# Norms in pieces, finished by GpSimd, in a four-layer transformer kernel; what a stage begins with is made by sequence in the preceding stage

## The chip, the cores and the metric

The kernel runs on one core of a Trainium2 chip, in one launch. The metric is the device time of that core in microseconds (us); lower is better. The core's engines run side by side, each with its own instruction queue: PE (TensorE, matrix products and transposes; PEld is its weight load), DVE (VectorE), ACT (ScalarE), POOL (GpSimd) and SP (SyncE, here a queue for transfers).

## The reference, cut to what matters

The input x is 4 sequences of 512 tokens with 128 channels, f32. There are four layers, and each of them does

```python
x = x + 0.5 * ffn(norm(x))
x = x + attn(norm(x))
x = x + 0.5 * ffn(norm(x))          # norm: (x - mean) / sqrt(var + 1e-5) over the 128 channels
```

- Layer 0: ffn is a mixture of 8 gelu-gated experts (top 2, limited capacity), attention has 16 heads with one projection for queries, keys and values.
- Layer 1: ffn is a dense gated chain with ternary weights (512 hidden units, a silu gate and two gelu products); attention is a running weighted mean (cumulative sums of exp(k) k and exp(k)) whose input is normalized a second time with gamma and beta.
- Layer 2: ffn is a mixture in which each of 8 experts chooses 256 of the 2048 tokens; attention is linear (elu + 1).
- Layer 3: ffn is a top-1 mixture of three-layer experts; attention is softmax with 16 heads.

## The kernel before, in words

x stays in SBUF as four tiles of 128 tokens by 128 channels for each of four sequences. Weights come by transfer ahead of their stage. A scheduler orders the instructions of each engine from the program's dependences and its own estimates; where the code wants another order, `after(ins, before, ...)` adds a dependence for the scheduler only, without a wait on the chip. `in_turn` does that for PE: between two settings of it all PE work is issued in the program's order, except in `out_of_turn()`. A generator is a piece of work that is cut into steps: `step(pieces, n)` advances the first of a list of generators by n steps, `run` finishes one. `latest["ins"]` is the newest instruction of the main chain, which `behind_latest` puts something behind.

**Norms.** `layer_norm` (L220) does a whole norm of one sequence on DVE: four `bn_stats` (L228), four `bn_aggr` (L230), `inverse_root` (L202) on a 128x4 tile, and four scalings `xn` (L240). `inverse_root` is 4 small instructions (v, i, y, h: L210 to L213) and three Newton steps of 3 instructions (t, t, y: L215 to L217). `twice=True` (layer 1's attention) adds a second inverse root. `norm_in_pieces` (L246) is the same, cut into steps, used in layer 0's attention. `transposed` (L268) makes the transposes of a norm on PE and copies them by ACT.

**Layer 0.** `l0_route` (L356) makes norms, router logits, softmax and the slots of half of the tokens (1024); `slack` adds empty steps. `l0_dispatch` scatters rows to slots by indirect transfers, `l0_experts` (L488) does up and down products of 8 experts per half, `l0_gather` (L574) gathers the results back by indirect transfers on POOL, paced by memsets. In the attention, `scores` (L838) does 256 blocks of 128 queries; `ops.row_max` is a product (smax) and a maximum on DVE (mp, L695), `ops.weigh` a second product (sexp) and an exponential on ACT. `begin(c)` makes the norm and transposes of sequence c, `take_apart` splits projected queries into bf16 parts on POOL (partsq, restq), and `load` brings these to the layout of the products by transfers (rows, queries).

**Layer 1.** `l1` (L977) works on pairs of sequences, twice (first and second ffn), so there are four rounds. A round is, for its two sequences, `first` (products p, tiles ha_a), `hidden` with weights th1 (products pb), `hidden` with th2 (products pc), and in the next round `leave` (product po, which also adds to x). Each 128x512 tile of activations is split into three bf16 parts, h, hr and hl (`Parts.take_apart`, L966); hl (L969) is on POOL for even o and on DVE for odd. Beside it, in steps: `begin(k, b)`, the norm xn_g and transposes ps_g of a sequence that comes next, and `attention(b)`, with norm xn_a, transposes ps_a, products pk, pka and pv, two scans, and transposes po_a.

**Layers 2 and 3.** `l2_ffn` and `l3_ffn` begin with a norm of each sequence, its transposes and router logits lg, in tiles that belong to the stage, then the softmax or the choice of all 2048 tokens. They end with transfers that bring the result (`yt`, in layer 2 also x) and adds to x. `l2_attn` and `l3_attn` begin with `begin(b)` or `enter(b)`, a norm and transposes of each sequence, and end with the residual of each sequence.

Of the kernel before, what the change touches and what calls it, by code (L numbers as in the profile page):

```python
# [9 lines left out]
F32 = mybir.dt.float32  # L10
# [73 lines left out]
def kernel(  # L84
# [117 lines left out]
    def inverse_root(var, n, name, bufs=4):  # L202


        def tmp(tag, dt=F32):
            return small.tile([P, n], dt, tag=f"ir_{tag}{n}", bufs=bufs, name=f"ir_{tag}_{name}")

        v, h, t, y = (tmp(i) for i in ("v", "h", "t", "y"))
        i = tmp("i", I32)
        nc.vector.tensor_scalar(v, var, EPS, None, op0=ALU.add)  # L210
        nc.vector.tensor_scalar(i, v.bitcast(I32), 1, None, op0=ALU.logical_shift_right)
        nc.vector.tensor_scalar(y.bitcast(I32), i, -1.0, float(0x5F3759DF), op0=ALU.mult, op1=ALU.add)
        nc.vector.tensor_scalar(h, v, -0.5, None, op0=ALU.mult)  # L213
        for _ in range(3):
            nc.vector.tensor_tensor(t, y, y, op=ALU.mult)  # L215
            nc.vector.tensor_tensor(t, t, h, op=ALU.mult)
            nc.vector.scalar_tensor_tensor(y, t, 1.5, y, op0=ALU.add, op1=ALU.mult)  # L217
        return y

    def layer_norm(pool, src, name, bufs=2, width=D, twice=False):  # L220
# [11 lines left out]
        if twice:  # L232

            v2 = small.tile([P, TT], F32, tag="ln_v2", name=f"v2_{name}")
            nc.vector.tensor_tensor(v2, rs, rs, op=ALU.mult)
            nc.vector.tensor_tensor(v2, v2, mv[:, :, 1], op=ALU.mult)
            r2 = inverse_root(v2, TT, f"2{name}")
            nc.vector.tensor_tensor(rs, rs, r2, op=ALU.mult)
# [7 lines left out]
    def norm_in_pieces(pool, src, name, bufs=1):  # L246

        st = small.tile([P, TT, 6], F32, tag="ln_st", name=f"st_{name}")
        mv = small.tile([P, TT, 2], F32, tag="ln_mv", name=f"mv_{name}")
        xn = pool.tile([P, TT, D], F32, tag="xn", bufs=bufs, name=f"xn_{name}")  # L250
        for t in range(TT):
            nc.vector.bn_stats(out=st[:, t, :], in_=src[:, t, :])
            if t % 2:
                yield
        for t in range(TT):
            nc.vector.bn_aggr(out=mv[:, t, :], in_=st[:, t, :])
        yield
        rs = inverse_root(mv[:, :, 1], TT, name)
        yield
        for t in range(TT):  # L260
            nc.vector.tensor_scalar(
                xn[:, t, :], src[:, t, :], mv[:, t, 0:1], rs[:, t : t + 1], op0=ALU.subtract, op1=ALU.mult
            )
            if t % 2:
                yield
        return xn
# [14 lines left out]
    def softmax(pool, lg, n, name):  # L281
# [7 lines left out]
        nc.vector.tensor_reduce(out=mx, in_=lg, axis=AX.X, op=ALU.max)  # L289
        nc.vector.tensor_tensor(sh, lg, wide(mx, NE), op=ALU.subtract)  # L290
        nc.scalar.activation(ex, sh, AF.Exp)
        nc.vector.tensor_reduce(out=sm, in_=ex, axis=AX.X, op=ALU.add)
        nc.vector.reciprocal(rc, sm)
        nc.vector.tensor_tensor(pr, ex, wide(rc, NE), op=ALU.mult)
        return pr

    def first_largest(pool, v, n, name, dt=F32):
# [6 lines left out]
        nc.vector.tensor_reduce(out=mx, in_=v, axis=AX.X, op=ALU.max)  # L304
        nc.vector.tensor_tensor(eq, v, wide(mx, NE), op=ALU.is_equal)
        nc.vector.tensor_tensor(eq, eq, first, op=ALU.mult)
        nc.vector.tensor_reduce(out=m2, in_=eq, axis=AX.X, op=ALU.max)
        nc.vector.tensor_tensor(oh, eq, wide(m2, NE), op=ALU.is_equal)
# [47 lines left out]
    def l0_route(wk, k, half, in_memory=True, slack=0):  # L356
# [9 lines left out]
        for i in range(8):  # L366
            nc.vector.bn_stats(out=st[:, i, :], in_=tiles[i])
            if i % 4 == 3 or slack:
                yield
        for i in range(8):  # L370
            nc.vector.bn_aggr(out=mv[:, i, :], in_=st[:, i, :])
        yield
        rs = inverse_root(mv[:, :, 1], 8, nm)
        if slack:
            yield
        for i in range(8):
            nc.vector.tensor_scalar(
# [7 lines left out]
        for h in range(2):  # L385
# [10 lines left out]
            nc.vector.tensor_copy(lgs[:, 4 * h : 4 * h + 4, :], lg)  # L396
            yield
        raw = softmax(wk, lgs, 8, f"r{nm}")
        yield
        m1 = first_largest(wk, raw, 8, f"a{nm}", BF16)  # L400
        yield
        rest = tmp([P, 8, NE], "rest")
        nc.vector.tensor_tensor(rest, raw, m1, op=ALU.mult)
        nc.vector.tensor_tensor(rest, raw, rest, op=ALU.subtract)
        m2 = first_largest(wk, rest, 8, f"b{nm}", BF16)
# [15 lines left out]
        nc.vector.scalar_tensor_tensor(kept[0], p1, float(C0), m1, op0=ALU.is_lt, op1=ALU.mult)  # L421
        nc.vector.tensor_tensor(row[:, 0], p1, place, op=ALU.add)
# [11 lines left out]
        nc.vector.tensor_tensor(gate[:, 0], raw, kept[0], op=ALU.mult)  # L434
        nc.vector.scalar_tensor_tensor(kept[1], p2, float(C0), m2, op0=ALU.is_lt, op1=ALU.mult)
        nc.vector.tensor_tensor(row[:, 1], p2, place, op=ALU.add)
        yield
        nc.vector.tensor_tensor(gate[:, 1], rest, kept[1], op=ALU.mult)
        for i in range(2):
            nc.vector.tensor_tensor(row[:, i], row[:, i], kept[i], op=ALU.mult)  # L440


        if not in_memory:

            pos = tmp([P, 2, 8, NE], "pos")
            for i, p in enumerate((p1, p2)):
                nc.vector.scalar_tensor_tensor(pos[:, i], p, 1.0, kept[i], op0=ALU.add, op1=ALU.mult)
            again = tmp([P, 8, NE], "again")
            nc.vector.tensor_tensor(again, pos[:, 1], kept[0], op=ALU.mult)
            nc.vector.tensor_tensor(pos[:, 1], pos[:, 1], again, op=ALU.subtract)  # L450
            nc.vector.tensor_tensor(pos[:, 0], pos[:, 0], pos[:, 1], op=ALU.add)
# [5 lines left out]
        nc.vector.tensor_reduce(out=rw, in_=row, axis=AX.X, op=ALU.add)  # L457
        nc.vector.tensor_scalar(idx, rw, float(T2), None, op0=ALU.add)
        nc.vector.tensor_reduce(out=gt, in_=gate, axis=AX.X, op=ALU.add)
        nc.vector.tensor_scalar(gt, gt, 0.5, None, op0=ALU.mult)  # L460
# [15 lines left out]

    latest = {}

    def behind_latest(ins):
        after(ins, latest["ins"], "not in front of work that its data would hold up")  # L480
# [93 lines left out]
    def l0_gather(wk, k, half, y_d, blanks=0):  # L574
# [6 lines left out]
        def pieces(s):  # L581
# [11 lines left out]
            for _ in range(4):  # L593
                yield
# [152 lines left out]
    def l0_attn(lp):  # L747
# [11 lines left out]
        def begin(c):  # L759
            xn = yield from norm_in_pieces(lp, x[:, c], f"a0_{c}")  # L760
# [52 lines left out]
        def prepare():  # L813
# [5 lines left out]
            for i in range(2):  # L819
# [3 lines left out]
                yield  # L823
            values(0)
# [13 lines left out]
        def scores(wk, rt, aside):  # L838
# [57 lines left out]
            take_apart(2, nc.gpsimd)  # L896
# [6 lines left out]
            for s4 in range(AHEAD // 4, 64 + 17):  # L903
                for half in range(2):
# [6 lines left out]
                    if (s4, half) == (45, 0):  # L911
                        aside.append(l0_route(rt, 1, 0, in_memory=False, slack=2))
# [11 lines left out]
                    if 0 < i < 17:  # L924
# [4 lines left out]
                        if slot == 3 and i < 15:  # L929
# [47 lines left out]
    def l1(aside, then):  # L977
# [3 lines left out]
        pieces = list(aside)  # L981

        with tc.tile_pool(name="l1f", bufs=1, reuse_waits="tile") as wk, \
             tc.tile_pool(name="l1a", bufs=2, reuse_waits="tile") as wa:

            def begin(k, b):
                nm = f"{k}_{b}"
                xn = layer_norm(wk, x[:, b], f"g{nm}")
                yield
# [8 lines left out]
            def first(k, b):  # L998
                nm = f"{k}_{b}"
                act[b] = Parts(wk, 4, "h", 4, f"a{nm}")  # L1000
                for o in range(4):
# [12 lines left out]
                    latest["ins"] = act[b].take_apart(o, nc.gpsimd if o % 2 == 0 else None)  # L1014
                    step(pieces)

            def hidden(k, b, w, sc, name):
                nm = f"{k}_{b}"
                given, act[b] = act[b], Parts(wk, 4, "h", 4, f"{name}{nm}")
                for o in range(4):  # L1020
# [8 lines left out]
                    latest["ins"] = act[b].take_apart(o, nc.gpsimd if o % 2 == 0 else None)  # L1029
                    step(pieces)  # L1030
# [22 lines left out]
            def attention(b):  # L1053
# [8 lines left out]
                xn = layer_norm(wa, x[:, b], f"a1_{b}", twice=True)  # L1062
                yield
# [22 lines left out]
                yield  # L1086
# [10 lines left out]
            for b in (0, 1):  # L1097
                run(begin(0, b))
            last = ()
            for k in range(2):  # L1100
                for p in ((0, 1), (2, 3)):
                    for b in p:
                        if last:
                            leave(*last.pop(0))
                            if k + p[0] and not (k == 1 and p[0] == 2):
                                pieces.append(attention((b + 2) % 4))
                        first(k, b)
                    for b in p:
                        hidden(k, b, th1, hs1, "b")
                    if (k, p[0]) == (0, 0):  # L1110
                        for r in pieces:
                            run(r)
                        pieces.clear()
                        then()
                    nk, nb = (k, 2) if p[0] == 0 else (k + 1, 0)
                    if nk < 2:
# [3 lines left out]
                    for r in pieces:  # L1120
                        run(r)
                    pieces.clear()
                    last = [(k, b) for b in p]
            for r in last:
                leave(*r)

# [14 lines left out]
    def l2_ffn(k):  # L1141
        W = D + NE
        with tc.tile_pool(name=f"l2f{k}", bufs=1, reuse_waits="tile") as wk:
# [7 lines left out]
            xd = dram.tile([T, W], F32, tag=f"xd2{k}", name=f"xd2_{k}")  # L1151
            sums_of[k, 0] = dram.tile([T, D], F32, tag=f"s{k}0", name=f"sum_{k}_0")
            xns = []
            lg = acc_bank([P, NT, NE], f"lg2_{k}")
            for b in range(B):
                xn = layer_norm(wk, x[:, b], f"c{k}_{b}", bufs=B, width=W)
                xns.append(xn)
                xT = transposed(wk, xn[:, :, :D], f"c{k}_{b}")
                for t in range(TT):
                    matmul(  # L1160
# [842 lines left out]
```

## Time and profile before

| | |
|---|---|
| time, median of 3 runs (lowest, highest) | 1688.43 us (1686.02, 1689.11) |
| profiled execution, time | 1685.38 us |
| profiled execution, span | 1683.3 us |
| mean granted clock of PE | 0.88 |
| instructions | 24707 |

The profile is of one execution. A window's row gives the span and then each engine's busy time in that stretch (with the number of instructions), the clock granted to PE (1 is full speed), the busy share of the DMA engines and the rate. In a timeline row the first number is the start, the second the duration; the bracket tells how long the engine had been idle and what released it. A row of groups ends with busy time, mean duration in ns, and the idle time before the group. The stages of the span, in us:

| stretch | stage |
|---|---|
| 0 to 181 | layer 0, first ffn (routing, then two halves of experts) |
| 181 to 436 | layer 0, attention |
| 436 to 580 | layer 0, second ffn |
| 580 to 872 | layer 1, four rounds: to 645, 727, 809, 872 |
| 872 to 992 | layer 2, first ffn (router to 888) |
| 992 to 1034 | layer 2, attention |
| 1034 to 1153 | layer 2, second ffn (router to 1048) |
| 1153 to 1290 | layer 3, first ffn (router to 1176) |
| 1290 to 1545 | layer 3, attention (entry to 1316) |
| 1545 to 1683 | layer 3, second ffn (router to 1563) |

### The profile page before, as it was taken

The numbers are of one execution on the slowest core, as the hardware profiler recorded it, in microseconds if no ns is written. First come the engines' busy times: TensorE is split into PE (matmuls) and PEld (weight loads), VectorE is DVE, ScalarE is ACT, GpSimd is POOL, SyncE is SP. The second block draws the span as 40 slices with busy tenths as digits, with TensorE's granted clock in tenths as the row PEclk, the third lists the DMA queues.
The fourth block names the chain that finished last, engine by engine and source line by source line (L and its number), as shares of the span: only waits on it lengthen the run. The fifth ranks groups of instructions, "written<-read, shape, count | busy, mean of one in ns | idle before, by whom it ended". The sixth has DMA issues, their size and how long they took to land.

```text
span 1683.3 us, 24707 instructions
## 1 busy us (share of the span) xinstructions
PE 1364.7 (81%) x8372; PEld 851.1 (51%) x8372; DVE 1036.7 (62%) x3225; ACT 666.1 (40%) x1411; POOL 563.3 (33%) x756
## 2 busy tenths in 40 slices
PE   3999889989899987979992637373785899998685
PEld 2898524334489834444551525253684233333685
DVE  5447677888445688989856357724214788884311
ACT  1333457767532323433320212020342377775242
POOL 0444245231345171313210631072684200100585
PEclk9999779999999998989995868575797599998698
DMA  8022211111311000004020230123543423310345
GB/s 318 30 62 61 49 44 52 49 42 33 119 59 47 21 23 36 1 1 188 15 63 27 36 66 26 30 40 84 177 148 120 95 52 71 69 33 22 102 183 187
DMA packets 97145, 121.26 MB, mean 72 GB/s; under 512 B 12224, under 2 KB 85429, under 8 KB 95482
## 3 DMA queue, kind: packets, MB, share of 16 engines
q1 hardware_dynamic: 76393, 69.84, 14.5%
q0 software_dynamic: 15968, 44.98, 9.0%
q10 hardware_dynamic: 4656, 4.86, 0.8%
q8 instruction: 66, 1.08, 0.3%
q14 instruction: 62, 0.50, 0.1%
HBM read 91.88 MB, written 27.79 MB: 71 GB/s over the span
## 4 chain that ended last, share of the span: by engine, by line
PE 60%; DVE 15%; POOL 8%; DMA 7%; issue 6%; ACT 2%; SPq 1%; POOLq 0%; ACTq 0%; DVEq 0%
PE pa L162 9%; PE av L162 7%; PE po L162 7%; PE smax L162 6%; PE sexp L162 6%; PE pc L162 5%; PE pb L162 4%; PE lg L162 2%; POOL y L1584 2%; DMA sum<-y,idx 2%; DVE mp L695 2%; POOL paced L334 2%; PE p3b L162 2%; PE p L162 1%; PE pq L162 1%
## 5 line engine op out<-in xcount | busy, mean ns | idle before, releaser
L695 DVE TENSOR_REDUCE mp<-smax 128x1 f32<-128x512 f32 (+1 forms) x512 | 326.5, 683 | 63.6 <-PE smax L162 61.4
L733 ACT ACTIVATE e<-sexp 128x512 f32<-128x512 f32 x512 | 272.0, 599 | 116.5 <-PE sexp L162 112.0
L162 PE MATMUL smax<-keys,queries 72*128 72x512 bf16 x512 | 204.1, 410 | 12.4 <-DMA queries<-rows_q 4.6
L162 PE MATMUL sexp<-queries,keys 75*128 75x512 bf16 (+1 forms) x512 | 195.7, 393 | 13.8 <-DVE mp L695 12.3
L520 ACT ACTIVATE gl<-pa 128x256 f32<-128x256 f32 x160 | 61.2, 383 | 157.9 <-PE pa L162 112.3
L162 PEld LDWEIGHTS <-th 128*128 128x128 bf16 x768 | 73.9, 96 | 97.1 <-issue 4.2
L162 PEld LDWEIGHTS <-queries 72*128 72x128 bf16 x512 | 52.3, 103 | 139.5 <-issue 88.3
L1533 POOL DMA_INDIRECT xg<-xd,src x46 | 46.8, 1018 | 175.0 <-DVE wi L1523 167.7
L521 DVE TENSOR_TENSOR hid<-pa,gl 128x256 f32<-128x256 f32 x160 | 67.1, 423 | 55.4 <-ACT gl L520 45.2
L162 PEld LDWEIGHTS po<-we,hid 128*128 128x128 f32 x768 | 90.5, 192 | 2.1
L162 PE MATMUL po<-we,hid 128*128 128x128 f32 x768 | 90.8, 275 | 0.0
L587 POOL DMA_INDIRECT yg<-y,idx x64 | 66.4, 1037 | 52.7 <-DMA y<-y 42.0
L162 PE MATMUL pa<-xTe,we 128*128 128x256 f32 (+1 forms) x352 | 81.7, 381 | 1.0 <-DVE xTe L509 1.0
L162 PE MATMUL pa<-ei,we 128*128 128x256 f32 (+1 forms) x352 | 81.3, 385 | 1.3 <-DVE hid L521 0.7
L162 PEld LDWEIGHTS <-keys 75*128 75x128 bf16 (+1 forms) x512 | 50.5, 101 | 55.5 <-issue 18.0
L162 PE MATMUL av<-e,v 128*32 128x512 f32 x512 | 72.6, 639 | 0.0
L334 POOL MEMSET paced<- 128x256 f32 x218 | 71.8, 329 | 0.3
L162 PEld LDWEIGHTS pa<-ei,we 128*128 128x128 f32 (+1 forms) x352 | 65.8, 192 | 10.7 <-DVE hid L521 1.4
L162 PEld LDWEIGHTS pa<-xTe,we 128*128 128x128 f32 (+1 forms) x352 | 64.5, 189 | 11.9 <-issue 1.4
L162 PE MATMUL av<-e,vp 128*32 128x512 f32 x512 | 69.6, 612 | 0.0
L165 PE MATMUL ps_a<-cst,xn_a 128*128 128x128 f32 x64 | 14.9, 354 | 58.0 <-DVE xn_a L240 58.0
L162 PE MATMUL p3b<-h3a,wd 128*128 128x128 f32 x480 | 60.3, 281 | 0.0
(428 smaller groups left out, 2915.0 us busy)
## 6 DMA issues: line engine op xcount, KB each, us to landing
we<-in_w0p_dram SPq DMA_DIRECT2D x8, 1080.0 KB
we<-in_e_pack_dram SPq DMA_DIRECT2D x8, 963.0 KB
queries<-rows SPq DMA_DIRECT2D x48, 96.0 KB
queries<-rows_q SPq DMA_DIRECT2D x48, 96.0 KB
y<-y SPq DMA_DIRECT2D x32, 128.0 KB
xd<-xn_c SPq DMA_DIRECT2D x8, 272.0 KB
slots<-zero ACTq DMA_DIRECT2D x2, 1024.0 KB
xs<-slots SPq DMA_DIRECT2D x16, 128.0 KB
```

The lines of the kernel that those rows point to most:

```text
L162: return turn_of(nc.tensor.matmul(*a, **k))
L165: return turn_of(nc.tensor.transpose(*a, **k))
L334: zeros = nc.gpsimd.memset(paced, 0.0)
L520: nc.scalar.activation(gl, pa[:, 0], AF.Gelu_apprx_tanh)
L521: latest["ins"] = nc.vector.tensor_tensor(hids[e][:, c, :], pa[:, 1], gl, op=ALU.mult)
L587: m = nc.gpsimd.indirect_dma_start(out=yg[:, t, i], out_offset=None, in_=y_d[:, :], in_offset=rows_in(idx[:, i, t : t + 1]), bounds_check= ...
L695: return nc.vector.tensor_reduce(out=self.mp[i][:, t, j], in_=s, axis=AX.X, op=ALU.max, negate=True)
L733: return e, nc.scalar.activation(e, s, AF.Exp, scale=scale)
L1533: m = nc.gpsimd.indirect_dma_start(out=xg[i], out_offset=None, in_=xd[:, :], in_offset=rows_at(src, i), bounds_check=T - 1, oob_is_err=False,)
L1584: m = nc.gpsimd.indirect_dma_start(out=y_d[:, :], out_offset=rows_at(to, i), in_=y, in_offset=None, bounds_check=T - 1, oob_is_err=False,)
```

## The change

- `inverse_root` and `norm_in_pieces` take an engine. With `eng=nc.gpsimd`, DVE does the statistics and v, i and y; GpSimd does h, the Newton steps (four instructions each instead of three) and the four scalings. The DVE part of these norms, of routing and of its softmax is issued through `behind`, which puts each instruction behind `latest["ins"]` for the scheduler.
- Layer 0: norms 2 and 3 of the attention and the route beside it are finished by GpSimd; the third block's queries are taken apart in the preparation and loaded at the start of the scores. Routing of the second half goes through `behind` too.
- Layer 1: norms of the second pair of the first ffn, all of the second ffn and all attention norms are in pieces and finished by GpSimd. Attention generators have lists of their own. hl is on POOL for all o where a round is not the first, and for even o only in product c of the first round, none earlier. The load of resident constants goes behind the first round's product c.
- A class `Router` does the first part of the ffns of layers 2 and 3 (store of x or of the norm, norm, transposes, logits) for one sequence; the preceding stage runs it (`r2.enter`, `r3.enter`), in layer 1's last round for sequences 0 and 1 on GpSimd. `l2_ffn` and `l3_ffn` issue all loads of their end first and then the adds, and call `then(b)` after each. Layer 2's and 3's attention norms go the same way.

The core of the diff:

```diff
-    def inverse_root(var, n, name, bufs=4):
+    def inverse_root(var, n, name, bufs=4, vector=None, eng=None):
...
+        on = eng or vector
+        on.tensor_scalar(h, v, -0.5, None, op0=ALU.mult)
         for _ in range(3):
+            on.tensor_tensor(t, y, y, op=ALU.mult)
+            on.tensor_tensor(t, t, h, op=ALU.mult)
+            if eng:
+                on.tensor_scalar(t, t, 1.5, None, op0=ALU.add)
+                on.tensor_tensor(y, y, t, op=ALU.mult)
+            else:
+                on.scalar_tensor_tensor(y, t, 1.5, y, op0=ALU.add, op1=ALU.mult)
...
+    def norm_in_pieces(pool, src, name, bufs=1, eng=None, twice=False, width=D, tag="xn"):
...
+            (eng or behind).tensor_scalar(
+                xn[:, t, :D], src[:, t, :], mv[:, t, 0:1], rs[:, t : t + 1], op0=ALU.subtract, op1=ALU.mult
             )
...
@@ layer 0, attention
-            xn = yield from norm_in_pieces(lp, x[:, c], f"a0_{c}")
+            xn = yield from norm_in_pieces(lp, x[:, c], f"a0_{c}", eng=nc.gpsimd if c > 1 else None)
...
-                        aside.append(l0_route(rt, 1, 0, in_memory=False, slack=2))
+                        aside.append(l0_route(rt, 1, 0, in_memory=False, slack=3, eng=nc.gpsimd))
...
@@ layer 1
+                xn = yield from norm_in_pieces(
+                    wk, x[:, b], f"g{nm}", bufs=2, eng=nc.gpsimd if k + b // 2 else None
+                )
+                for _ in range(4):
+                    yield
...
-                    latest["ins"] = act[b].take_apart(o, nc.gpsimd if o % 2 == 0 else None)
-                    step(pieces)
+                    low = k or b > 1 or name == "c" and o % 2 == 0
+                    latest["ins"] = act[b].take_apart(o, nc.gpsimd if low else None)
+                    go_on()
...
-                xn = layer_norm(wa, x[:, b], f"a1_{b}", twice=True)
-                yield
+                xn = yield from norm_in_pieces(wa, x[:, b], f"a1_{b}", bufs=2, eng=nc.gpsimd, twice=True)
+                for _ in range(2):
+                    yield
...
+                            if (k, p[0]) == (1, 2):
+                                pieces.append(enter(b - 2, nc.gpsimd))
+                            else:
+                                attending[b % 2].append(attention((b + 2) % 4))
...
+            for k, b in last:
+                run(enter(b))
...
@@ routers of layers 2 and 3
+        def enter(self, b, eng=None):
...
+            xT = transposed(nxt, xn[:, :, :D], nm, bufs=B)
+            yield
+            lg = acc_bank([P, TT, NE], f"lg{nm}")
+            for t in range(TT):
+                matmul(
+                    lg[:, t, :], lhsT=xT[:, t * P : (t + 1) * P], rhs=take(mat, MAT, f"wr{layer}"),
+                    start=True, stop=True,
+                )
...
@@ layer 3, attention
+                    if slot == 0 and i in (2, 6):
+                        enters.append(l3_enter(xTs, i // 4 + 2, nc.gpsimd))
+                    with out_of_turn():
+                        step(aside if i >= 16 else enters)
...
@@ the stages in their order
-    l2_ffn(0)
-    l2_attn()
-    l2_ffn(1)
+    begin, rest = l2_attn()
+    l2_ffn(0, r2, lambda b: begin(b) if b == 0 else None)
+    r2 = Router(1, 2)
+    rest(r2.enter)
+    r3 = Router(0, 3)
+    l2_ffn(1, r2, lambda b: run(r3.enter(b)))
     early.close()
-    l3_ffn(0)
+    xTs = {}
+    l3_ffn(0, r3, lambda b: run(l3_enter(xTs, b)) if b == 0 else None)
     late.close()
+    r3 = Router(1, 3)
     with psum_of("att3"):
-        l3_attn()
+        l3_attn(xTs, r3.enter)
```

## The prediction

> **What bounds the kernel now.** I read the head of the profile's page first.
>
> ```profile
> span 1683.3 us, 24707 instructions
> PE 1364.7 (81%) x8372; PEld 851.1 (51%) x8372; DVE 1036.7 (62%) x3225; ACT 666.1 (40%) x1411; POOL 563.3 (33%) x756
> PEclk9999779999999998989995868575797599998698
> ```
>
> PE is busy for 81%, so 318 us of idle is all that a reordering can win, and POOL, to which the change moves work, has the most room. The clock row falls to .5 to .7 where a stage begins. The windows by stage say where the idle time lies (columns: span, then PE, weight loads, DVE, ACT, POOL, clock, DMA).
>
> ```profile
> 580.00:645.00 65.00, 58.34 (x256) 25.60 (x257) 53.91 (x125) 20.60 (x29) 35.49 (x44) 0.97 0.13 41
> 645.00:727.00 82.00, 71.02 (x401) 35.55 (x399) 70.94 (x195) 30.96 (x41) 19.11 (x17) 0.94 0.00 1
> 809.00:872.00 63.00, 62.73 (x406) 32.07 (x403) 42.38 (x98) 18.95 (x26) 13.26 (x13) 1.00 0.04 12
> 872.00:888.00 16.00, 11.01 (x48) 9.01 (x48) 10.15 (x61) 3.94 (x6) 0.00 (x0) 0.62 0.57 155
> 1034.00:1048.00 14.00, 11.36 (x48) 9.46 (x48) 8.25 (x57) 2.34 (x4) 0.00 (x0) 0.58 0.07 19
> 1545.00:1563.00 18.00, 12.99 (x58) 10.72 (x56) 9.78 (x59) 2.93 (x5) 0.00 (x0) 0.59 0.21 59
> ```
>
> Layer 1's first pair of sequences (580:645) idles 6.7 us, its second and third pair 11 each, its last 0.3. The three short rows are router entries: PE at about .6 clock, POOL idle. The waits and the timeline name what PE waits for.
>
> ```profile
> PE ps_a L165 <- DVE xn_a L240: 58.0, 10, 24.3
> 662.73 1.16 PE L165 MATMUL ps_a<-cst,xn_a 128*128 128x128 f32 x4 [8.01 <-DVE xn_a L240]
> 232.30 0.59 PE L162 MATMUL sexp<-queries,keys 75*128 75x512 bf16 x1 [4.86 <-DVE mp L695]
> 230.53 1.11 DVE L261 TENSOR_SCALAR xn_a<-x,mv_a,ir_y_a 128x128 f32<-128x128 f32 x4
> 231.56 2.48 DVE L695 TENSOR_REDUCE mp<-smax 128x1 f32<-128x512 f32 x4
> ```
>
> In layer 1 PE waits 8.01 us for a norm; in layer 0's attention it waits 4.86 us for four maxima that stood on DVE behind a whole norm.
>
> **Price of a norm.** On DVE: 4 statistics of .28, 4 aggregates of .16, 13 dependent small operations at .20 spacing and 4 scalings at .26 (1.11 for four): 1.1 + .6 + 2.6 + 1.1 = 5.4 us. GpSimd takes the last ten small ones and the scalings, 3.1 us off DVE. There the multiply-add is two instructions, so 13 small ones. No 128x4 arithmetic runs on POOL before. The nearest rows:
>
> ```profile
> L1173 POOL TENSOR_SCALAR xn_c<-pr_c 128x32 f32<-128x32 f32 x8 | 2.8, 364 | 42.8 <-DVE pr_c L294 42.8
> L1249 POOL COPY px<-cst 128x8 f32<-128x8 f32 x2 | 0.4, 198 | 11.0 <-DVE st_c L228 11.0
> 655.47 1.52 POOL L969 TENSOR_TENSOR hl_a<-hr_a 128x512 bf16<-128x512 f32 x1 [2.10 <-DVE ir_t_a L215]
> 655.99 1.02 DVE L216 TENSOR_TENSOR ir_t_a<-ir_t_a,ir_h_a 128x4 f32<-128x4 f32 x1
> ```
>
> From .16 (DVE's own) to .40 (the first rows' mean rounded up, .364), and a two-input instruction of one engine is seen to stretch beside one of the other: hl_a 1.52 instead of 1.04, a 128x4 product 1.02 instead of .16. I take .27, near the .25 spacing of four 128x32 scalings (1.42 us in all, the first .66) with a little for the stretch. A norm's finish on POOL is then 13 x .27 + 4 x .4 = 5.1 us; layer 1's double norm, 29 small ones, 7.8 + 1.6 and two hops to DVE, about 10.
>
> GPSIMD Engine Reference, 4.1, speaks against the move: elementwise work belongs on VectorE, GpSimd being about twice as slow with two inputs. Beside hl, 1.04 on POOL against .69 on DVE, that is 1.5 here. By twice DVE's .20, an estimate from that page, the small operation would cost .40 and the sum below would end at +5 instead of -17. SBUF — State Buffer, "Who interferes with whom", calls the ports that DVE and GpSimd share an exclusive lock, which the two stretched rows agree with; by it the moved operations would queue in layer 1, where DVE is busy 71 of 82 us.
>
> **Layer 0, experts.** Routing of the second half goes behind the first half's expert products. The first expert starts some 5 us sooner (its position matrix waited 2.1 us behind the other half's logits copy, with about 2 us of the other half's norm on DVE and its logits on PE), but 5.8 us of PE work (transposes 2.2, logits 1.7 and 1.9) enters a stretch where PE is busy 60.4 of 61 us. Net +1. The 16 dispatch transfers (1.47 each, 23.5 on POOL) end about 12 us before the half is needed; without that cover each us late costs one. The entry of the second FFN, with four waits of .34 to .7, -1. Together 0 (-4 to +3).
>
> **Layer 0, attention.** Norms 2 and 3 and the next route leave DVE in pieces behind the newest maximum; the third block is taken apart and loaded ahead of the scores. The stalls 4.86, 4.80 (behind the route's eight scalings, 2.74) and 1.06 should go; the 2.88 at 191 waits for row transfers and may. What comes late next is POOL's parts-to-rows-to-queries chain: 5 to 6.5 us of norm stand ahead of it, against 4.5 to 6 us of slack per block of 12.5. So not all of these 13.6: -8 (-13 to -2).
>
> The pieces' place behind the newest maximum is an order for the scheduler and no wait: it costs nothing by itself, but a norm that is placed later makes its transposes later.
>
> **Layer 1.** Gathers of layer 0's result wait longer and are stepped with blanks; the second pair's norms stand between them on POOL (1.47 per gather and its pacing fill). By PE's order the transposes of g_2 stand at the eighth group of product b (nominal 612, ready 614 to 617), of g_3 after the first group of c on the second sequence (632 to 635, ready 636 to 638). Before, g waited 5.46. The first pair's hl of products a and b move from POOL, busy 35.5 of 65 us with the gathers, to DVE, busy 53.9: 8 times .69 more there, covered by what the two norms take off it (6.2) and no more. -2 (-5 to +3). The constants that layer 1's attention reads are loaded after hidden c instead of b, about 21 us before use: nothing, and one for one beyond that cover.
>
> Pairs 2 and 3: PE now places two groups of b (2.7 each) ahead of the attention's transposes. Walked from the pair's first instruction at 0: PE reaches ps_a_0 at 21.4, its double norm is ready near 25.7 (stall 4.4, then .9 for the key product); ps_a_1 at 36.1 against 38.3 (2.2 and .9); .6 before the last transposes; about 1.8 at ps_g_0: 10.8 with POOL at .25, against 11.0 before. POOL also takes all hl of b and c, 16 a pair instead of 8, 8.3 us, and DVE gives up 5.5. Behind a waiting POOL norm then stand hl and so PE's next product. At .27 I put +2 for both pairs (-12 with the stalls gone, +14 where POOL lags).
>
> Pair 4 had no idle time. It gets two router sequences: 4 us of transposes and logits, warm or nearly so, and a wait at ps_r_0 (reached near 12, ready near 17) that displaces what was no stall. Some products run beside it: +4 (0 to +8).
>
> **Entries.** The router of layer 2 took 3.55 us per sequence at half clock (transposes 1.1, copy .73, logits 1.88). After pair 4 two of four legs are left behind the last norm: 11 instead of 16.8 us, -5. Layer 2 attention and its second router are DVE-bound (39.2 of 42, then 8.25 of 14): three legs go inside, the last norm and leg remain (about 10 after the last residual): -4 (-9 to 0). Layer 3's attention tail takes one leg into the scores and one before the last projection; the last norm is no longer covered by three legs, about 10 instead of 14.8, less 2 of PE work: -3 (-6 to 0). Each router sequence also issues on SP the store of its normalized rows, in layer 2 that of its sums too, at .3 to .4 us of SP; in layer 3's tail that stands before the query loads, of which the last block's (1.37 of PE waiting at 1532) is past by then: 0. "All loads in front": SP's order of these loads and of the final stores is the same as before, and after layer 2's first FFN the adds already follow each other at .8: 0. Layer 3's attention entry gets its first norm at most 1 us sooner before three chained row transfers: -1. Sum -13 (-21 to -3).
>
> **Sum.** 0 - 8 - 2 + 2 + 4 - 13 = -17 against the profiled execution, 1685.38 (span 1683.3 and 2.1 around it): 1668.4. The median of the runs, 1688.43, stands 3.0 above it: 1671.
>
> **Rivals.** *GpSimd finishes too late (slower).* Place: ps_a, ps_g and ps_r in layer 1, which PE's order puts at a fixed point whether the norm is there or not. Price: each .01 us more per small operation is 58 of them a pair, in two pairs, plus four single norms and the two of pair 4, about 1.7 us. Break-even with -17 at .37 us; at .40, +5 (1693), at .45 1701. For it: DVE busy 71 of 82 and the stretched rows; against it: POOL is busy only 19 of those 82. *GpSimd is as quick as DVE.* At .18, -15 more: 1656; the 198 ns copy speaks for it. *The entries don't shrink*: the last sequence's chain and the transfers behind it end the stage as before, and only the middle counts: -4, 1684. For it: the loads keep their order, and the legs moved inside take time on a DVE that is full.
>
> **Chances.** Forecast .47 (1659 to 1680), GpSimd late .20, GpSimd quick .18, entries unchanged .15. A measurement tells some .2% (3.4 us) from nothing. Faster: .47 + .18 + half of .15 = .73; same .10 (the other half and a little of the late case); slower .17. The range 1648 to 1697 reaches from the quick case with layer 0's best end to the late case at .42.
>
> **What would show it.** Right: POOL rows of 128x4 at .25 to .3; 232's stall gone; ps_a waits of 4 and 2 us; entries of 10 to 11 us. Wrong: POOL rows above .37 or ps_a waits over 8 (late); second and third pair under 76 us (quick); router entries still near 15 (unchanged); a wait for queries on PE in layer 0's attention.

## The result and the profile after

The changed kernel takes 1763.49 us (median of 4 runs, 1757.43 to 1775.94) against 1687.22 for the kernel before: a ratio of 1.0463, 95% interval 1.0397 to 1.0529. It is slower, and 92 us above the forecast. The profiled execution took 1757.43 us. The head of its page:

```profile
span 1755.6 us, 24767 instructions
PE 1390.8 (79%) x8372; PEld 856.6 (49%) x8372; DVE 974.7 (56%) x2927; ACT 668.7 (38%) x1413; POOL 709.2 (40%) x1129
```

DVE gave up 62 us and POOL took on 146, so the work that moved is more than twice as dear there. Where the time went is seen by cutting both traces at the same products (a stage runs from the start of its first product to that of the next stage's; all in us):

| stage | before | after | change | forecast |
|---|---|---|---|---|
| layer 0 up to the attention's first score | 161.1 | 160.0 | -1.1 | 0 (with the second ffn) |
| layer 0, attention | 265.7 | 246.1 | -19.6 | -8 |
| layer 0, second ffn | 153.6 | 152.9 | -0.7 | |
| layer 1, round 1 | 64.6 | 79.1 | +14.5 | -2 |
| layer 1, rounds 2 and 3 | 162.3 | 206.2 | +43.8 | +2 |
| layer 1, round 4 | 58.9 | 85.0 | +26.1 | +4 |
| last residuals to layer 2's ranking | 23.3 | 22.7 | -0.6 | -5 |
| layer 2, first ffn to the first norm behind it | 110.0 | 108.2 | -1.8 | 0 |
| layer 2, attention and second router | 51.4 | 63.6 | +12.2 | -4 |
| layer 2, second ffn | 110.0 | 107.6 | -2.4 | 0 |
| layer 3, first router | 16.5 | 20.3 | +3.8 | 0 |
| layer 3, first ffn | 120.5 | 116.4 | -4.1 | 0 |
| layer 3, attention and second router | 266.0 | 268.7 | +2.7 | -4 |
| layer 3, second ffn | 119.2 | 118.8 | -0.4 | 0 |

Layer 1, with the entry to layer 2, goes from 309.1 to 393.1: it alone loses 84 us. The windows of its rounds 1, 2 and 4 after (columns as in the prediction):

```profile
559.02:638.15 79.13, 66.21 (x257) 27.26 (x257) 47.27 (x103) 20.60 (x29) 40.80 (x70) 0.85 0.10 34
638.15:741.74 103.59, 80.30 (x374) 35.84 (x372) 54.87 (x104) 30.81 (x40) 61.19 (x123) 0.88 0.00 1
844.30:929.34 85.04, 73.73 (x362) 37.87 (x361) 30.95 (x65) 20.02 (x28) 35.27 (x55) 0.84 0.02 7
```

In round 2, cut the same way before, PE was busy 69.5 of 80.5 us at a clock of .94. Now it idles 23.3 instead of 11.0, and its products also take 10.8 us more, at .88. The groups on POOL show the price that the forecast had to guess:

```profile
L290 POOL TENSOR_SCALAR xn_a<-x,mv_a,ir_y_a 128x128 f32<-128x128 f32 x32 | 25.7, 811 | 0.9
L290 POOL TENSOR_SCALAR xn_g<-x,mv_g,ir_y_g 128x128 f32<-128x128 f32 x24 | 19.3, 810 | 0.5
L241 POOL TENSOR_SCALAR ir_t_a<-ir_t_a 128x4 f32<-128x4 f32 x24 | 6.2, 257 | 2.1
L242 POOL TENSOR_TENSOR ir_y_a<-ir_y_a,ir_t_a 128x4 f32<-128x4 f32 x24 | 4.8, 199 | 2.0
```

A scaling takes .81 us, where .4 had been put. A small operation is near the forecast .27 only when it is alone. The timeline of round 2, first POOL and DVE:

```profile
655.08 0.20 POOL L242 TENSOR_TENSOR ir_y_a<-ir_y_a,ir_t_a 128x4 f32<-128x4 f32 x1
655.35 0.73 POOL L238 TENSOR_TENSOR ir_t_a<-ir_y_a 128x4 f32<-128x4 f32 x1
656.16 0.20 POOL L239 TENSOR_TENSOR ir_t_a<-ir_t_a,ir_h_a 128x4 f32<-128x4 f32 x1
656.45 0.65 POOL L241 TENSOR_SCALAR ir_t_a<-ir_t_a 128x4 f32<-128x4 f32 x1
...
659.11 0.99 DVE L214 TENSOR_SCALAR ir_v_2a<-v_a 128x4 f32<-128x4 f32 x1 [2.09 <-POOL v_a L284]
...
666.99 3.14 POOL L290 TENSOR_SCALAR xn_a<-x,mv_a,ir_y_a 128x128 f32<-128x128 f32 x4
...
677.25 0.17 DVE L214 TENSOR_SCALAR ir_v_2a<-v_a 128x4 f32<-128x4 f32 x1 [11.22 <-POOL v_a L284]
```

A small operation starts .28 to .31 after the last one when it is alone, and is stretched to .65 or .73 beside DVE's 128x512 splits. Over layer 1's 12 norms the 220 small operations come to .44 us each, counted from the first one to the first scaling with the hops to DVE and the hl in between, and to .38 without the hops. A single norm's finish took 7.7 to 11.2 us there, a double norm's 15.1 to 17.9; 5.1 and about 10 were forecast. The double norm hands over to DVE in its middle, and there DVE, at the head of whose queue the hop stands, waits 2.09 us with all its other work behind. At the second norm's hop it waits 11.22; DVE's next work after that hop, a split of hr_b, had to wait for ACT until 678.67, so the longer wait held up little. Then PE:

```profile
667.85 0.48 PE L165 MATMUL ps_a<-cst,xn_a 128*128 128x128 f32 x1 [6.08 <-POOL xn_a L290]
668.63 0.47 PE L165 MATMUL ps_a<-cst,xn_a 128*128 128x128 f32 x1 [0.31 <-POOL xn_a L290]
669.41 0.48 PE L165 MATMUL ps_a<-cst,xn_a 128*128 128x128 f32 x1 [0.30 <-POOL xn_a L290]
670.18 0.47 PE L165 MATMUL ps_a<-cst,xn_a 128*128 128x128 f32 x1 [0.30 <-POOL xn_a L290]
671.52 2.07 PE L162 MATMUL pk<-hT,mat 128*128 128x512 f32 x2 [0.87 <-ACT hT L1118]
673.39 0.64 PE L162 MATMUL pb<-ha_a,th 128*128 128x512 bf16 x1
673.82 0.63 PE L162 MATMUL pb<-hr_a,th 128*128 128x512 bf16 x1
...
683.74 0.33 PE L165 MATMUL ps_a<-cst,xn_a 128*128 128x128 f32 x1 [1.44 <-POOL xn_a L290]
...
722.96 0.33 PE L165 MATMUL ps_g<-cst,xn_g 128*128 128x128 f32 x1 [2.78 <-POOL xn_g L290]
```

Each transpose waits for its own scaling, so four take 2.8 us instead of .6 to 1.2. The 6.08 is not what is new: before, PE waited 8.01 at the same transposes. New are 3.3 us of waits at the second attention norm (1.44, .45, .45, .93) and 4.1 and 2.6 at the two norms of the next round (ps_g), where before no wait was over .4. Behind the 6.08 of idling the products of b start .43 apart, where they start .22 apart at full clock: the granted clock is .50 from 668 to 676. TensorE: Matmul & The Clock Gate of the Trainium skill, Part 1, gives the rule that an idle window of some 3.4 us halves the clock and as long a busy one restores it. The row agrees with the first half; here it is still down at 675.1, 7 us after PE went on, with small waits in between.

### The profile page after: what moved, and what is told of

Its sections match the earlier page's. It is cut to its first block, busy times and chain, and to the rows that moved or that the text cites. A ratio compares the mean times of both kernels' runs of the same rounds, so it can differ in the third digit from the quotient of the medians.

```text
span 1755.6 us, 24767 instructions
## 1 busy us (share of the span) xinstructions
PE 1390.8 (79%) x8372; PEld 856.6 (49%) x8372; DVE 974.7 (56%) x2927; ACT 668.7 (38%) x1413; POOL 709.2 (40%) x1129
## 3 DMA queue, kind: packets, MB, share of 16 engines
q10 hardware_dynamic: 4656, 4.86, 0.8%
## 4 chain that ended last, share of the span: by engine, by line
PE 54%; DVE 15%; POOL 15%; DMA 6%; issue 5%; ACT 2%; SPq 2%; POOLq 0%; DVEq 0%; ACTq 0%
PE pa L162 8%; PE po L162 6%; PE av L162 6%; PE smax L162 6%; PE sexp L162 6%; PE pc L162 4%; PE pb L162 2%; DMA sum<-y,idx 2%; POOL y L1665 2%; PE p3b L162 2%; POOL paced L363 1%; PE pq L162 1%; POOL xg L1614 1%; PE lgr L162 1%; POOL wd L1625 1%
## 5 line engine op out<-in xcount | busy, mean ns | idle before, releaser
L162 PEld LDWEIGHTS <-th 128*128 128x128 bf16 x768 | 79.4, 103 | 114.0 <-issue 32.1
L545 ACT ACTIVATE gl<-pa 128x256 f32<-128x256 f32 x160 | 61.3, 383 | 154.1 <-PE pa L162 113.0
L162 PEld LDWEIGHTS pa<-xTe,we 128*128 128x128 f32 (+1 forms) x352 | 64.6, 189 | 11.8 <-issue 1.4
L498 POOL DMA_INDIRECT slots<-xn,idx x32 | 31.5, 985 | 85.7 <-DVE idx L214 80.7
L1360 POOL DMA_INDIRECT xg<-xd,idx x32 | 31.4, 981 | 86.0 <-DVE junk L1341 78.1
```

What stands on the lines that cost most here:

```text
L162: return turn_of(nc.tensor.matmul(*a, **k))
L498: m = nc.gpsimd.indirect_dma_start(out=slots_of[half][:, :], out_offset=rows_in(idx[:, i, t : t + 1]), in_=xn[:, t, :], in_offset=None, bo ...
L545: nc.scalar.activation(gl, pa[:, 0], AF.Gelu_apprx_tanh)
L1360: m = nc.gpsimd.indirect_dma_start(out=t, out_offset=None, in_=xd[:, :], in_offset=rows_at(e, h))
```

## The experiments

Ratios are to the kernel before on the same chip; chips differ by 1%, so stage times of different experiments are compared as such only for layers 0 to 2 and layer 3's first router. There the same code repeats within about 3 us (the layer 1 of the kernel before took 309.0 to 311.8 in six profiles), except in layer 0's attention (last section). The expectations of e1 to e4 give times for a kernel before that takes 1687; on their chip it took 1705, so their measured ratios are put on 1687 here. "Layer 1" is from its first transposes to layer 2's ranking: 309.1 before, 393.1 after.

**Layer 1 as before (e1).**

```diff
-    def l1(aside, then, enter):   # changed
+    def l1(aside, then, enter):   # the function of the kernel before, and behind its last leave:
+            for b in range(B):
+                run(enter(b))
```

> The changed kernel with layer 1 written as before (whole norms on DVE, hl alternating, old lists of pieces and old gather; all four routers of layer 2's first ffn after the last residual). Stage by stage the changed kernel is 21.5 us ahead at the first transposes of layer 1, loses 84 us from there to layer 2's ranking, and about 10 behind it. If layer 1 alone carries the loss: 1763 - 84 = 1679, that is 8 below the kernel before. If the stages only look separate (a clock or a transfer that layer 0 leaves late): above 1700.

Measured: 0.9998 (0.9970 to 1.0025), or 1687, 8 above the expected 1679, as much as the entry behind layer 1 grew. Layer 1 is 319.2, of which its four rounds take 288.3 (285.7 before) and the entry 30.9 instead of 23.3. The loss of layer 1 is its own: 73.9 of the 84 us come back. The gain of layer 0 is eaten up by the entries and layer 2's attention (63.5 again).

**DVE instead of GpSimd, and the place of hl (e2, e3, e4).**

```diff
@@ e2
-                    wk, x[:, b], f"g{nm}", bufs=2, eng=nc.gpsimd if k + b // 2 else None
+                    wk, x[:, b], f"g{nm}", bufs=2, eng=None
-                xn = yield from norm_in_pieces(wa, x[:, b], f"a1_{b}", bufs=2, eng=nc.gpsimd, twice=True)
+                xn = yield from norm_in_pieces(wa, x[:, b], f"a1_{b}", bufs=2, eng=None, twice=True)
-                                pieces.append(enter(b - 2, nc.gpsimd))
+                                pieces.append(enter(b - 2, None))
@@ e3 (e4: both)
-                    latest["ins"] = act[b].take_apart(o, nc.gpsimd if o % 2 == 0 and (k or b > 1) else None)
+                    latest["ins"] = act[b].take_apart(o, nc.gpsimd if o % 2 == 0 else None)
-                    low = k or b > 1 or name == "c" and o % 2 == 0
+                    low = o % 2 == 0
```

> The changed kernel with no GpSimd finish in layer 1 (norms still in pieces, behind the newest split, on DVE). Theory P (GpSimd's finish is too long: scalings of .79 us, 26 or more small operations): the stalls at ps_a, ps_g and ps_r shrink and most of the 84 us comes back, 1690 to 1710. Theory H (all hl on GpSimd, or all on DVE in the first round, holds PE up): 1745 or more. Theory O (the place of the transposes in PE's order holds PE up whoever makes the norm): 1740 or more.

> The changed kernel with hl on GpSimd for even o and on DVE for odd o in every round, as before; norms still finished by GpSimd. Theory P: at most 15 us better, 1748 to 1763, since GpSimd has 8 us of hl less per round. Theory H: 1690 to 1710. Theory O: 1755 or more.

> Both edits: layer 1's norms in pieces but on DVE, hl alternating. Differs from the layer 1 of before only in where the pieces are put. P or H or both: 1680 to 1700. Theory O: 1740 or more, since the order alone would hold PE up.

Measured: e2 1.0073 (1.0049 to 1.0098), e3 1.0415 (1.0364 to 1.0466), e4 1.0088 (1.0060 to 1.0116). On the scale of 1687 that is 1699.5, 1757 and 1702. With the norms on DVE layer 1 is 330.5: 62.6 of the 84 us come back. Moving hl back gives 5.0 (e3, 388.1) or takes 3.5 (e4, 334.0), little more than the same code varies. Theory P holds, H does not, and O's 1740 with norms on DVE was not seen; but e4 is 2 us above its range, and e11 below shows that the new places do cost something. Round 2 of e2 from its own windows:

```profile
623.97:711.43 87.46, 72.19 (x368) 34.69 (x372) 69.18 (x185) 30.36 (x40) 26.55 (x24) 0.92 0.00 1
```

DVE is as busy as before, and PE idles 15.3, 8 less than with GpSimd; its products are 8 us quicker. PE's wait for the first attention norm is no shorter with that norm on DVE:

```profile
655.16 1.15 PE L165 MATMUL ps_a<-cst,xn_a 128*128 128x128 f32 x4 [7.51 <-DVE xn_a L214]
```

What went are the waits at the second attention norm and at ps_g, none of them over .4 here.

**Which part of the finish (e8, e9, e10; the code shortened).**

```diff
@@ e8: the changed kernel, layer 1's scalings on DVE
-            (eng or behind).tensor_scalar(xn ...
+            behind.tensor_scalar(xn ...
@@ e9: the kernel of e2, layer 1's scalings on GpSimd
-            behind.tensor_scalar(xn ...
+            nc.gpsimd.tensor_scalar(xn ...          # not the routers'
@@ e10: layer 1's attention norms alone
-                ... f"a1_{b}", bufs=2, eng=nc.gpsimd, twice=True)
+                ... f"a1_{b}", bufs=2, eng=None, twice=True)
```

> The changed kernel with layer 1's four scalings per norm on DVE and the Newton steps still on GpSimd. The scalings took .79 us each on GpSimd and pace the transposes (2.8 us for four). If they are the main part of layer 1's loss: 40 us or more comes back, ratio 1.015 to 1.023. If the chain of small operations with its hops between the engines is: 8 to 20 us, 1.034 to 1.042 (changed kernel 1.046).

> The mirror of e8: in layer 1 the Newton steps on DVE and the four scalings on GpSimd (routers wholly on DVE). If scalings and steps cost about what e8 and e2 give (37 us for the scalings, 25 to 30 for the chain) and add up, this one loses the 37 less what round 4 has no share in: ratio 1.020 to 1.030 (e2: 1.007). If the two only hurt together (GpSimd full): 1.008 to 1.015.

> The changed kernel with only the doubly normalized attention norms of layer 1 on DVE; the norms of the next round's sequences and of the router stay on GpSimd. The four attention norms have 29 small operations and two hops each, the others 13 and none. If the long chain is what hurts: rounds 2 and 3 come to 88 to 92 us (103 in the changed kernel), ratio 1.024 to 1.034. If each scaling hurts alike, wherever: 4 of 12 norms, 1.032 to 1.040.

Measured: e8 1.0256 (1.0203 to 1.0310), e9 1.0206 (1.0181 to 1.0230), e10 1.0365 (1.0336 to 1.0394). e8 fell between its two ranges, nearer that of the scalings: layer 1 is 355.8, so the scalings cost 37.3 of the 62.6, the steps 25.3. e9 agrees roughly: 353.7, 23.2 more than e2 with no scaling of a router among them; in e8 the scalings of rounds 1 to 3 cost 27.1. The two parts add up roughly, so it is not a GpSimd that is full, which e9's round 2 shows too: POOL busy 38.9 of 94.7 us, and PE idle 21.3.

```profile
631.60:726.30 94.70, 73.38 (x368) 34.21 (x373) 66.75 (x170) 30.82 (x40) 38.88 (x40) 0.93 0.00 1
```

e10's time fell in the "each scaling alike" range, not where the long chain was expected. But the shares are not alike: layer 1 is 383.2, 9.8 less, where 4 of 12 norms would have 20.9 of the 62.6. With the attention norms alone on DVE, PE waits 7.54 us for the first of them, and the waits for GpSimd at ps_g stay:

```profile
678.50 1.15 PE L165 MATMUL ps_a<-cst,xn_a 128*128 128x128 f32 x4 [7.54 <-DVE xn_a L214]
```

So by e2 and e10 52.8 of the 62.6 come back only when the single norms leave GpSimd too: the long chain of the attention norms is not the main part.

**Pieces or places (e11).**

```diff
-                xn = yield from norm_in_pieces(wk, x[:, b], f"g{nm}", ...)
+                xn = layer_norm(wk, x[:, b], f"g{nm}")
-                xn = yield from norm_in_pieces(wa, x[:, b], f"a1_{b}", ..., twice=True)
+                xn = layer_norm(wa, x[:, b], f"a1_{b}", twice=True)
-                                pieces.append(enter(b - 2, nc.gpsimd))
+                                pieces.append(enter(b - 2, None))
```

> The changed kernel with whole norms on DVE in layer 1, not in pieces and not behind the newest split, at the new places. e2 and e4 lose 12 to 15 us to e1 with DVE norms. If cutting them into pieces behind the newest split does that: rounds 2 and 3 at 81 to 83 us, ratio 0.998 to 1.003. If the new places of the steps (and the two routers in round 4) do: rounds 2 and 3 at 86 to 91, 1.005 to 1.012.

Measured: 1.0020 (0.9998 to 1.0042), inside the first range by its time, but rounds 2 and 3 took 87.7 and 86.6, the second theory's. Layer 1 is 325.0. Of e2's 21.4 over the kernel before, the pieces have 5.5, little more than the same code varies, and the new places 15.9: round 1 -3.7, rounds 2 and 3 +11.9, round 4 with its two routers +8.3, the entry -0.6. The ranges for the time and for the rounds did not fit each other: e1, from which the time was taken, has rounds of 81 to 82 but an entry that is 8.2 us longer than here. Which of the new places costs what within rounds 2 and 3 was not taken further and stays open.

**Router adds that wait for PE (e7), router steps inside layer 2's attention (e13).** In layer 3's first router of the changed kernel DVE and PE read:

```profile
1235.26 0.19 DVE L1231 TENSOR_TENSOR lb<-lgr,rws 128x32 f32<-128x32 f32 x1 [1.70 <-PE lgr L162]
...
1236.65 1.24 PE L165 MATMUL ps_r<-cst,xn_r 128*128 128x128 f32 x4 [1.42 <-DVE xn_r L214]
1238.57 1.88 PE L162 MATMUL lgr<-mat,xT_r 128*128 128x8 f32 x8 [0.67 <-ACT xT_r L303]
```

The add of one sequence's logits waits on DVE for PE; the next norm's last steps stand behind it, and PE then waits for that norm.

```diff
@@ e7: the kernel of e1, and
-            nc.vector.tensor_tensor(self.lb[:, b * TT : (b + 1) * TT], lg, br, op=ALU.add)
+            nc.scalar.copy(self.lb[:, b * TT : (b + 1) * TT], lg)     # one add of br for all, ahead of the softmax
@@ e13: the kernel of e7, and in layer 2's attention
-            enters.append(then(b))
-            if b < B - 1:
-                step(enters[b:], 6)
-            if b:
-                run(enters[b - 1])
-        run(enters[B - 1])
+        for b in range(B):
+            run(then(b))
```

> The kernel of e1 (layer 1 as before, the rest changed), where each sequence's router logits are copied out by ACT and the bias is added once by DVE ahead of the softmax or choice, in place of an add per sequence on DVE. Theory W (an add that waits for PE's logits stands at the head of DVE's queue and holds the next sequence's norm): the entry after layer 1 gets 4 to 7 us shorter, layer 3's first router 3 to 4, layer 2's attention 3 to 6; 10 to 15 us in all, ratio 0.991 to 0.995 (e1: 0.9998). Rival (the entries are long because the legs take PE and DVE time wherever they stand): at most 3 us, 0.998 or more.

> The kernel of e7 with layer 2's second router run after the attention's last residual instead of in steps inside it. In e7 the stretch from layer 2's attention to its second ranking is 61.3 us, in the kernel before 51.4. If the legs inside hold the attention up: 51 to 54, ratio 0.987 to 0.990 (e7: 0.994). If it is the pieces' norm or the early begin of sequence 0: 58 or more, 0.992 or more.

Measured: e7 0.9939 (0.9915 to 0.9962), e13 0.9881 (0.9861 to 0.9902). In e7 the entry behind layer 1 goes from 30.9 to 27.5, layer 3's router from 20.3 to 16.7, layer 2's attention from 63.5 to 61.3: 9 us, and PE's router legs follow each other without a wait for a norm:

```profile
1164.01 1.20 PE L165 MATMUL ps_r<-cst,xn_r 128*128 128x128 f32 x4
1165.89 1.87 PE L162 MATMUL lgr<-mat,xT_r 128*128 128x8 f32 x8 [0.68 <-ACT xT_r L309]
1167.61 1.09 PE L165 MATMUL ps_r<-cst,xn_r 128*128 128x128 f32 x4
```

So the wait is shown, at the low end: the ratio is in its range, the entry and layer 2's attention came back less than expected. e13 settles the rest of layer 2's attention: with the legs behind it the stretch is 50.0 instead of 61.3. Windows of that stretch, the changed kernel and e13:

```profile
1060.20:1123.80 63.60, 43.85 (x208) 33.26 (x208) 45.86 (x207) 15.92 (x26) 6.43 (x6) 0.74 0.06 17
```

```profile
987.10:1037.10 50.00, 38.66 (x209) 30.50 (x210) 43.63 (x204) 16.83 (x30) 6.31 (x6) 0.81 0.07 22
```

The same DVE work, 45.9 and 43.6 us, needs 63.6 or 50.0: DVE was not the bound. With the legs inside, two chains that go from DVE to PE, to ACT and back stand in one queue. DVE's waits for PE and ACT are 13.9 us in e7's stretch and 5.3 in e13's, which is 8.6 of the 11.3 between these two kernels.

**Layer 0 alone, and GpSimd's share in it (e5, e6, e14, e15).**

```diff
@@ e5: layer 0 changed, layers 1 to 3 as before; e6: e5, and e14: e12 (below; e15 is e12 again), with
-            xn = yield from norm_in_pieces(lp, x[:, c], f"a0_{c}", eng=nc.gpsimd if c > 1 else None)
+            xn = yield from norm_in_pieces(lp, x[:, c], f"a0_{c}", eng=None)
-                        aside.append(l0_route(rt, 1, 0, in_memory=False, slack=3, eng=nc.gpsimd))
+                        aside.append(l0_route(rt, 1, 0, in_memory=False, slack=3, eng=None))
```

> Layer 0 of the changed kernel (GpSimd finish, pieces behind the newest maximum, third block loaded ahead, second half's route behind the experts), and layers 1 to 3 of the kernel before. By the stages of the changed kernel, layer 0 is 21.5 us shorter: ratio 0.987 to 0.989 to the kernel before. If that time is given back behind layer 0 (layer 1 waits for a transfer that is no earlier): 0.995 or more.

> As e5, but the norms and the route in layer 0's attention are finished on DVE; pieces, their place behind the newest maximum and the early load stay. Theory G (the gain comes from the work that GpSimd takes off DVE): half of the 20 us or more is lost, ratio 0.994 or more. Theory B (it comes from cutting the norm into pieces that stand between maxima, and from the early load): 0.987 to 0.991.

> The kernel of e12 with layer 0's norms and route finished on DVE. e5 and e6 differed by 0.45% with wide intervals. If GpSimd's finish is worth something in layer 0: 4 to 9 us slower than e15 on the same chip, by the attention's length 2 to 11 us. If e5 and e6 differed by chance: within 3 us of e15.

> e12 again, on the chip of e14, to compare with: ratio 0.981 to 0.986.

Measured: e5 0.9903 (0.9876 to 0.9930), e6 0.9948 (0.9927 to 0.9969), e14 0.9937 (0.9919 to 0.9956), e15 0.9856 (0.9835 to 0.9878). e5 missed its range of 0.987 to 0.989: its profile has 254.8 us in the attention, where the changed kernel had 246.1 (last section). GpSimd's finish is worth 8 us by e5 and e6 (.45% of 1703; 7 by the medians), which theory G expected. By e14 and e15 it is worth 14 (.81% of 1687; 10 by the medians), more than the 4 to 9 expected; in their profiles the attention takes 262.0 and 250.2. Both theories hold in part: the pieces and the early load alone keep 4 (e14's attention, 262.0 for 265.7) to 9 us (e6), and GpSimd brings the rest.

**A version that beats both (e12).** Layer 0 of the changed kernel, layers 1 and 2 of the kernel before, layer 3 of the changed kernel with e7's edit.

```diff
-    l1(aside, residents, r2.enter)            # changed layer 1
+    l1(aside, residents, None)                # layer 1 before
-    rest(r2.enter)
-    l2_ffn(1, r2, lambda b: run(r3.enter(b)))
+    l2_attn()                                 # layer 2 before
+    l2_ffn(1, lambda b: run(r3.enter(b)))
```

> Layer 0 of the changed kernel, layers 1 and 2 of the kernel before, layer 3 of the changed kernel with the router's logits copied by ACT and one bias add. From e5 (0.990) and, by its stages, 4 to 5 us less in layer 3's first ffn and 1 to 2 in its attention (e7): 0.985 to 0.988. If those stages vary only by run: 0.989 to 0.991.

Measured: 0.9834 (0.9814 to 0.9854), 1657.57 against 1687.05, a little better than forecast; e15, the same kernel on another chip, 0.9856.

## Why the prediction was wrong, point by point

- **Price of a norm.** The step that failed first: the finish on GpSimd was put at 5.1 us for a norm and took 7.7 to 11.2 in layer 1, and at about 10 for a double norm, which took 15.1 to 17.9. Both terms were too low. The small operation, put at .27, is near that alone, but came to .38 on average and .44 with the hops. The scaling was put at .4, from a row of a quarter of its columns and with one constant operand, and took .81 with two operands that differ by partition, three times DVE's .26. Four take 3.1 us instead of 1.6, and PE's transposes wait for them one by one. By e8 the scalings are 37 of layer 1's 84 us and the steps 25; by e11 the pieces are 5.5 and the new places 15.9.
- **GPSIMD Engine Reference** of the Trainium skill, 4.1, calls GpSimd's elementwise work about twice as slow with two inputs and near the line rate with one. The scaling, with one tile input, took three times DVE's: here the measurement decides. With the lock of SBUF — State Buffer, "Who interferes with whom", the .65 and .73 beside a usual .20 agree.
- **Rounds 2 and 3 of layer 1.** The walk had the place of the first stalls right (4.4 forecast, 6.08 measured; 2.2 forecast, 1.44 and three more of .45 to .93). It was wrong on two counts. PE idled 23.3 us instead of 10.8: at ps_g 6.7 instead of 1.8, at the attention's last transposes 2.6 instead of .6, and 1.7 at the first products. And it counted idle time alone, while the products slowed by 10.8 us as well; a price per .01 us that was worked out from stalls had to come out too low by that.
- **Round 1, round 4.** Two norms and two router norms, -2 and +4 forecast, +14.5 and +26.1. Round 1 stalls 5.08 and 5.13 at ps_g (before, one stall of 5.46), round 4 4.93 and 3.72 at ps_r, each with 2.8 us of transposes and a clock of .85 and .84 over the round. That PE had other products to do did not help: its order put the transposes in front of them, whether the norm was there or not, as the rival said.
- **Rivals.** "GpSimd finishes too late" is what happened, at .20, in the place it named. Its break-even of .37 us per small operation was reached, at .38 to .44; but its price of 1693 to 1701 for such operations is far under 1763, since it held the scaling at .4 and left out the slower products. Its own count, 116 operations in double norms and 78 in single ones, also makes 1.9 us per .01, not 1.7. "The entries don't shrink" came as well, and worse than its -4.
- **Layer 0.** The stalls of 4.86, 4.80 and 1.06 went, as forecast; -19.6 instead of -8, and -10.3 to -21.5 in other profiles of the same code. "Not all of these" was too careful: POOL's chain did become late, in waits for rows of .9 to 2.4 and one for queries of 1.5, but the clock came up. These are the stretches that held the two long stalls, before and after:

```profile
222.00:262.00 40.00, 34.80 (x169) 11.67 (x162) 28.87 (x78) 21.63 (x41) 12.86 (x22) 0.79 0.17 45
342.00:382.00 40.00, 33.61 (x196) 12.63 (x188) 34.31 (x87) 23.76 (x47) 12.12 (x21) 0.91 0.18 44
```

```profile
222.00:262.00 40.00, 37.71 (x310) 15.50 (x308) 31.78 (x78) 30.25 (x66) 22.66 (x47) 1.00 0.23 60
342.00:382.00 40.00, 38.81 (x245) 15.63 (x238) 33.64 (x83) 29.21 (x58) 17.77 (x40) 1.00 0.17 45
```

  In this attention PE's idle time fell by 10.0 us and its busy time by 9.6; in layer 1's four rounds the first rose by 42.0 and the second by 42.5, two routers' products among it. So a us of idling went with about one more of slow products, as a gain and as a loss, and the 318 us of idle were not all that a reordering can win.
- **Entries.** -13 forecast, +12.2 from layer 2's attention alone. The step from a stage that is DVE-bound to legs that are covered inside it failed: DVE's share was high, but the stage was a chain (e13). That every add per sequence is one more wait at the head of DVE's queue was in the diff and not in the working (e7: 9 us). The entry to layer 2 gave .6 instead of 5: with all four legs behind the last residual it takes 30.9 (e1), 27.5 without those waits (e7) and 23.3 in the old form, and what the other 4 us are stays open. Layer 3's attention gained nothing that shows: the new code took 262.1 to 268.7 in the profiles, the old 263.5 to 266.0. The orders of the final loads and stores were the same, and layer 3's end changed by -0.4, as forecast.

## What to carry to other kernels

Price an operation on another engine by a row with the same kind of operands, and if there is none, put the break-even on that operation too. Count a stall of PE with the slow products behind it, both when it goes and when it comes. GpSimd's slow finish is a gain where the result is needed some stages later (layer 0's attention) and a loss where PE's order puts its reader into the same round; an instruction that waits for another engine is also a wait for everything behind it.

## What the runs showed of the hardware

- A GpSimd scaling of 128x128 f32 with mean and root per partition takes .81 us, while a GpSimd copy of 128x512 bf16 takes .61 and a two-input product of 128x512 1.04 in the same kernel.
- Layer 0's attention of the same code took 246.1 (changed kernel), 249.1 (e12), 254.8 (e5) and 255.4 us (e10) in profiled executions, with a granted clock of 1.00, .91, .84 and .83 in the stretch from 262 to 302 us. In all four PE stalls once there, for 2.25 to 2.62 us near 285, while it waits for rows. The same stall lowered the clock of that stretch by nothing up to a sixth; what decides that was not tried.
